# A third set of expert weights on chip, placed over finished token residuals, in an attention and mixture-of-experts kernel

## The chip, the cores and the metric

The kernel runs on one core of one Trainium2 chip. The metric is device microseconds (us) for one execution of the whole program. A core has five engines with a queue of instructions each: PE multiplies matrices, DVE (vector), ACT (scalar) and POOL (GpSimd) work element by element, and SP only issues transfers. A transfer (DMA) is issued by an engine's queue and then carried out by 16 DMA engines that all queues share. Each queue runs its instructions in order: an instruction that waits holds up all that stand behind it.

## What is computed

The input is 2048 tokens of 512 channels (8 sequences of 256). First a long convolution of key-value products with a query, summed per head, is added to x. Then comes a mixture of 16 experts, of which each token takes four, at most 256 tokens to an expert, and a shared expert that all tokens take. Cut to what matters:

```python
x = x + ssm_attention(ctx, ctx, layernorm(x), ssm_kernel, D)
h = layernorm(x)                                   # (2048, 512)
scores = softmax(h @ gate_w.T); topk_w, topk_i = top_k(scores, 4)
buf, wbuf = tokens and weights of each expert      # (16, 256), the rest is padding
xg   = h[buf]                                      # gather
mid  = silu(xg @ w_gate) * (xg @ w_up)             # (16, 256, 352)
eout = (mid @ w_down) * wbuf                       # (16, 256, 512)
y    = zeros.at[buf].add(eout)                     # scatter with addition
x    = x + y + (silu(h @ sw_gate) * (h @ sw_up)) @ sw_down
```

All numbers are f32.

## The kernel before

The order of the instructions of each engine is the order in which the program writes them; nothing is moved by a scheduler.

**The attention.** `xs` (line 102) keeps the residual x of all 16 tiles of 128 tokens in SBUF, [128, 16, 512]. A loop over the 16 tiles (line 724) computes the attention and adds it to `xs`. The shared expert is written as generators (`shared_block`, line 142): pieces of its work are put between other work with `fill(count)`. For a tile it ends with an addition to `xs` (line 195) and a transfer from there to `out` (line 196). After that the tile of `xs` isn't read again. The tiles are finished in the order 1, 0, 2, 3 and then in pairs (line 699).

**The routing** (lines 858 to 963) runs while the shared expert's last blocks (tiles 10 to 15) fill PE. In it the weights of experts 0 and 1 are asked for (line 936, four transfers each on SP's queue: gate, up, and down in two parts; `load_expert`, line 845), and later the table of the routing weights, `prob`, is written to DRAM beside the normalised tokens (`xw_d<-prob`, line 957, SP's queue). The gathers read that table too.

**An expert's tokens** take this way: `find` (line 906) computes its list of tokens on PE and DVE. `gather` (line 965) issues two indirect transfers on POOL's queue. `shuffle` (line 976) sends the result to DRAM (`slots`) and fetches it in another order (`gb`, four transfers), on SP's queue, each waiting for the one before. `tokens` (line 989) turns it on DVE to `xgT`. Three experts' tokens are under way at once (AHEAD is 3).

**The expert loop** (line 1095) does, for expert e: `gate_up` (PE, ACT, DVE); `pack` of expert e+1 (line 1002: ACT copies the columns of its last, narrow block to `wt`, so it waits for that expert's gate and up weights); `tokens(e+1)`; `find` and `gather` of expert e+3; `down` twice (line 1063), once for each half of the 256 slots. Each `down` ends with a scaling to `eo_sb` on DVE (three buffers) and an indirect transfer on POOL's queue that adds to `out` in DRAM (line 1076); below it is called the scatter. The scatters all write `out`, so each of them waits until the one before has landed. At the end of the iteration SP gets the loads of expert e+2 and then `shuffle` of expert e+3:

```python
        if e + 2 < E:
            experts[e + 2] = load_expert(e + 2)
        if e + AHEAD < E:
            moved[e + AHEAD] = shuffle(gathered[e + AHEAD])
```

The weights stand in a pool of two buffers (line 838), so the load of e+2 goes where expert e was, and waits for PE's `gate_up` and `down` of e.

Of the kernel before, what the change touches and what calls it, by code (L numbers as in the profile page):

```python
# [8 lines left out]
F32 = mybir.dt.float32  # L9
# [11 lines left out]
P = 128  # L21
BK = 32
B, S, L = 8, 256, 512
HD = 8
NC = L // P
# [5 lines left out]
E, K, CAP, I, IS = 16, 4, 256, 352, 704  # L31
# [22 lines left out]
def ssm_attention__then__moe_kernel(  # L54
# [47 lines left out]
    xs = keep.tile([P, NT, L], F32, name="xs")  # L102
# [157 lines left out]
    with ExitStack() as att:  # L260
# [441 lines left out]
        def fill(count):  # L702
            while count and behind:
                try:
                    next(behind[0])
                    count -= 1
                except StopIteration:
                    behind.pop(0)
# [15 lines left out]
        for n in range(NT):  # L724
            more = n + 1 < NT
            swift = n + 1 in SWIFT
            t = seq[n]
# [110 lines left out]
    wpool = ctx.enter_context(tc.tile_pool(name="wpool", bufs=2))  # L838
# [3 lines left out]

    NI = -(-I // P)

    def load_expert(e):
        w = wpool.tile([P, 2, NC, I], F32, name="w")
        wd = wpool.tile([P, NI, L], F32, name="wd")
        full = I // P * P
        nc.sync.dma_start(out=w[:, 0], in_=w_gate[e].rearrange("(p c) f -> p c f", p=P))
        nc.sync.dma_start(out=w[:, 1], in_=w_up[e].rearrange("(p c) f -> p c f", p=P))  # L850
        nc.sync.dma_start(
            out=wd[:, 0 : I // P, :], in_=w_down[e, 0:full, :].rearrange("(c p) f -> p c f", p=P)
        )
        nc.sync.dma_start(out=wd[0 : I - full, I // P, :], in_=w_down[e, full:, :])
        return w, wd
# [32 lines left out]
            tok.unsqueeze(2).broadcast_to([P, NT, E, 3]),  # L888
        )

    AHEAD = 3
    idx = route.tile([P, E, NSL], I32, name="idx")
    ido = route.tile([P, E, NSL], I32, name="ido")

    def compare(e):

        hot = ffn.tile([P, NT, P], BF16, name="hot", bufs=1)
        nc.vector.tensor_tensor(
            hot,
            pos[:, :, e : e + 1].broadcast_to([P, NT, P]),  # L900
            slot_f.unsqueeze(1).broadcast_to([P, NT, P]),
            ALU.is_equal,
        )
        return hot

    def find(e, hot):


        ip = ps_sm.tile([P, NSL * 3], F32, name="ip", tag="sm")
        for i in range(NT):  # L910
            nc.tensor.matmul(
                ip,
                lhsT=hot[:, i, :],
                rhs=what[:, i, e].rearrange("p n k -> p (n k)"),
                start=(i == 0),
                stop=(i == NT - 1),
            )
        info = route.tile([P, NSL, 3], F32, name="info", bufs=2)
        nc.vector.tensor_copy(info, ip.rearrange("p (n k) -> p n k", k=3))
        who = route.tile([P, NSL], F32, name="who", bufs=2)  # L920
        gap = route.tile([P, NSL], F32, name="gap", bufs=2)
        nc.vector.tensor_scalar(gap, info[:, :, 2], -1.0, 1.0, ALU.mult, ALU.add)
        nc.vector.scalar_tensor_tensor(
            who, info[:, :, 0], float(S), info[:, :, 1], ALU.mult, ALU.add
        )

        nc.vector.scalar_tensor_tensor(
            info[:, :, 1], gap, float(S), info[:, :, 1], ALU.mult, ALU.add
        )
        nc.vector.scalar_tensor_tensor(  # L930
            ido[:, e, :], info[:, :, 1], float(B), info[:, :, 0], ALU.mult, ALU.add
        )
        nc.vector.tensor_mul(gap, gap, empty)
        nc.vector.tensor_add(idx[:, e, :], who, gap)  # L934

    experts = {e: load_expert(e) for e in range(2)}
    fill(1)
    hots = {0: compare(0)}

# [18 lines left out]
    fill(2)  # L958
    for e in range(1, AHEAD):
        hots[e] = compare(e)  # L960
        fill(3)
        find(e, hots.pop(e))
    hots[AHEAD] = compare(AHEAD)

    def gather(e):
        g = ffn.tile([P, NSL, ROW], F32, name="g", bufs=AHEAD - 1)
        for n in range(NSL):
            nc.gpsimd.indirect_dma_start(  # L968
                out=g[:, n, :],
                out_offset=None,  # L970
                in_=xw_d[:, :],
                in_offset=bass.IndirectOffsetOnAxis(ap=ido[:, e, n : n + 1], axis=0),
            )
        return g

    def shuffle(g):


        slots = dram.tile([CAP, L], F32, name="slots", bufs=2)
        nc.sync.dma_start(out=slots.rearrange("(n q) f -> q n f", n=NSL), in_=g[:, :, 0:L])  # L980
        gb = ffn.tile([P, NSL * NB, P], F32, name="gb", bufs=AHEAD - 1)
        for i in range(NB):
            nc.sync.dma_start(
                out=gb[i * BK : (i + 1) * BK],
                in_=slots[:, i * P : (i + 1) * P].rearrange("(j b) f -> b j f", b=BK),
            )
        return gb

    def tokens(e):

        gb, g = moved.pop(e), gathered.pop(e)
        wg = ffn.tile([P, NSL], F32, name="wg")
        for n in range(NSL):
            nc.vector.tensor_copy(wg[:, n : n + 1], g[:, n, L + e : L + e + 1])
        xgT = ffn.tile([P, NC, CAP], F32, name="xgT")
        for n in range(NSL):
            transpose_blocks(xgT[:, :, n * P : (n + 1) * P], gb[:, n * NB : (n + 1) * NB])
        return xgT, wg
# [3 lines left out]
    def pack(w):  # L1002

        wt = ffn.tile([P, NC, 6 * Q], F32, name="wt", bufs=1)
        a, b = NW * P, NW * P + 2 * Q
        for lo, cols in ((0, slice(a, b)), (P, slice(b, I))):
            n = cols.stop - cols.start
            nc.scalar.copy(
                wt[:, :, lo : lo + 2 * n].rearrange("p c (k f) -> p c k f", k=2),
                w[:, :, :, cols].rearrange("p k c f -> p c k f"),  # L1010
            )
        return wt
# [50 lines left out]
    def down(e, n, mid, wd, wg):  # L1063
        po = ps_ex.tile([P, L], F32, name="eo", tag="ex")
        for k, f in enumerate((NW, *range(NW))):
            m = min(P, I - f * P)
            nc.tensor.matmul(  # L1067
                po,
                lhsT=mid[:m, f, n * P : (n + 1) * P],
                rhs=wd[:m, f, :],  # L1070
                start=(k == 0),
                stop=(k == NW),
            )
        o = ffn.tile([P, L], F32, name="eo_sb", bufs=3)
        nc.vector.tensor_scalar_mul(o, po, wg[:, n : n + 1])  # L1075
        nc.gpsimd.indirect_dma_start(  # L1076
            out=out,
            out_offset=bass.IndirectOffsetOnAxis(ap=idx[:, e, n : n + 1], axis=0),
            in_=o,
            in_offset=None,  # L1080
            compute_op=ALU.add,
        )

    gathered, moved = {}, {}
    for e in range(AHEAD - 1):
        gathered[e] = gather(e)
# [3 lines left out]
    wt_next = pack(experts[0][0])  # L1090
    gathered[AHEAD - 1] = gather(AHEAD - 1)
    moved[AHEAD - 1] = shuffle(gathered[AHEAD - 1])
    while behind:
        fill(1)
    for e in range(E):
        w, wd = experts.pop(e)
        wt = wt_next
        xgT, wg = xgT_next
        mid = ffn.tile([P, NI, CAP], F32, name="mid")
        if e + 1 < E:  # L1100
            gate_up(xgT, mid, w, wt, slice(0, CAP))
            wt_next = pack(experts[e + 1][0])
            xgT_next = tokens(e + 1)
            if e + AHEAD < E:
                find(e + AHEAD, hots.pop(e + AHEAD))
                gathered[e + AHEAD] = gather(e + AHEAD)
            for n in range(NSL):
                down(e, n, mid, wd, wg)
            if e + AHEAD + 1 < E:
                hots[e + AHEAD + 1] = compare(e + AHEAD + 1)  # L1110
        else:

            gate_up(xgT, mid, w, wt, slice(0, P))
            gate_up(xgT, mid, w, wt, slice(P, CAP), (NW,))
            down(e, 0, mid, wd, wg)
            gate_up(xgT, mid, w, wt, slice(P, CAP), range(NW))
            down(e, 1, mid, wd, wg)
        if e + 2 < E:
            experts[e + 2] = load_expert(e + 2)
        if e + AHEAD < E:  # L1120
            moved[e + AHEAD] = shuffle(gathered[e + AHEAD])

# [37 lines left out]
```

## Time and profile before

| | us |
|---|---|
| three runs: median, lowest, highest | 694.14, 691.29, 695.07 |
| the profiled execution, its own time | 693.31 |
| its span, first to last instruction | 691.6 |
| PE busy (matmuls) | 657.2 (95%) |
| weight loads of PE busy | 488.1 (71%) |
| DVE, ACT, POOL busy | 386.1, 185.1, 314.8 |

The times of the trace below are in microseconds from the start of the span. The attention lasts until about 357, the routing with the rest of the shared expert until 423, the sixteen experts until the end. The DMA engines move 117.79 MB, 170 GB/s on average over the span. An expert's weights are 704 + 704 + 512 + 192 KB, 2112 KB together. A group's line in the page has the line of the code, the engine, what is written and read, the count, and the time; a line of waits has who waited, for what, and then the total in us, how often, and the longest. In the timeline the number in brackets is the idle time of the engine before the instruction, and what ended it.

### The profile page before, as it was taken

To read this page: it belongs to the slowest core of one execution; us is meant where nothing else is said; L and a number is where in the kernel's file an instruction comes from. 1 tells how busy PE (TensorE), PEld (TensorE's weight loads), DVE (VectorE), ACT (ScalarE), POOL (GpSimd) and SP (SyncE) were. 2 spreads that over 40 slices of the span, in tenths; PEclk is the share of its full clock that TensorE was granted. 3 is DMA by queue.
4 is the path that set the end of the run, shared out by engine and by line. 5 is a ranking of instruction groups with operands and counts; after the bars stand their busy time and mean duration, and the time that the engine had idled before them with its cause. 6 is when DMAs were issued, how large, how long until landed. Compare 5 with 4: busy or idle time off the path is not lost. (4 is left out here: it accounts for less than half of the span.)

```text
span 691.6 us, 9761 instructions
## 1 busy us (share of the span) xinstructions
PE 657.2 (95%) x3310; PEld 488.1 (71%) x3310; DVE 386.1 (56%) x932; ACT 185.1 (27%) x465; POOL 314.8 (46%) x477
## 2 busy tenths in 40 slices
PE   7889999998999999999999999999999999899891
PEld 5667977777867877877868686766677777676670
DVE  4946666878877776676645611455455444443320
ACT  2454343444342342422322010111111111111110
POOL 5667547777685676546210310223344333332121
PEclk9999999999999999999999999999999999999997
DMA  5783454555557535441018461698999999889943
GB/s 128 244 234 99 130 160 110 159 134 149 147 143 181 146 94 150 113 108 45 16 59 274 122 188 31 207 264 254 260 267 257 254 254 251 250 254 279 266 85 44
DMA packets 98438, 117.79 MB, mean 170 GB/s; under 512 B 11267, under 2 KB 64355, under 8 KB 98388
## 3 DMA queue, kind: packets, MB, share of 16 engines
q1 hardware_dynamic: 90932, 99.86, 48.9%
q0 software_dynamic: 7168, 17.04, 12.5%
q10 hardware_dynamic: 288, 0.26, 0.3%
q8 instruction: 26, 0.43, 0.3%
q14 instruction: 24, 0.20, 0.1%
HBM read 84.25 MB, written 32.88 MB: 169 GB/s over the span
## 5 line engine op out<-in xcount | busy, mean ns | idle before, releaser
L468 PE MATMUL y<-kv,toep 128*128 128x288 f32 x528 | 140.9, 411 | 3.1 <-DVE f L518 2.7
L468 PEld LDWEIGHTS y<-kv,toep 128*128 128x128 f32 x528 | 100.0, 192 | 34.6 <-issue 7.7
L1076 POOL DMA_INDIRECT out<-eo_sb,idx x32 | 56.2, 1756 | 147.1 <-DMA wd<-in_L_ffn_w_down 73.6
L1025 PE MATMUL pgu<-xgT,w 128*128 128x256 f32 (+1 forms) x544 | 113.5, 367 | 0.0
L1025 PEld LDWEIGHTS pgu<-xgT,w 128*128 128x128 f32 x544 | 98.6, 190 | 12.9 <-issue 0.5
L1067 PE MATMUL eo<-wd,mid 128*128 128x512 f32 (+1 forms) x192 | 86.4, 598 | 0.0
L520 POOL TENSOR_TENSOR f<-f 128x256 f32<-128x256 f32 x60 | 43.8, 729 | 92.7 <-DVE f L518 87.4
L445 POOL TENSOR_TENSOR kv<-k 128x256 f32<-128x256 f32 x126 | 84.9, 706 | 0.0
L168 PE MATMUL sgu<-xnT,swg 128*128 128x256 f32 (+1 forms) x400 | 78.4, 339 | 0.4 <-DVE tail L162 0.4
L168 PE MATMUL sgu<-xnT,swu 128*128 128x256 f32 (+1 forms) x400 | 77.9, 338 | 0.0
L968 POOL DMA_INDIRECT g<-xw_d,ido x32 | 36.7, 1146 | 85.4 <-DVE idx L934 43.8
L185 PE MATMUL so<-swd,smid 128*128 128x512 f32 x160 | 73.9, 593 | 0.0
L168 PEld LDWEIGHTS sgu<-xnT,swg 128*128 128x128 f32 x400 | 65.8, 192 | 8.1 <-DVE tail L162 0.6
L168 PEld LDWEIGHTS sgu<-xnT,swu 128*128 128x128 f32 x400 | 64.6, 191 | 6.3
L1067 PEld LDWEIGHTS eo<-wd,mid 128*128 128x128 f32 (+1 forms) x192 | 35.2, 189 | 38.1 <-issue 34.8
L1033 DVE TENSOR_TENSOR mid<-eact,pgu 128x256 f32<-128x256 f32 (+1 forms) x34 | 13.8, 406 | 75.9 <-ACT eact L1032 72.8
L491 DVE TENSOR_TENSOR y<-y,again 128x576 f32<-128x576 f32 x28 | 21.4, 766 | 57.7 <-PE y L468 44.8
L185 PEld LDWEIGHTS so<-swd,smid 128*128 128x128 f32 x160 | 29.9, 190 | 31.9 <-issue 30.4
L177 ACT ACTIVATE act<-sgu 128x256 f32<-128x256 f32 (+1 forms) x50 | 17.1, 341 | 123.4 <-PE sgu L168 123.4
L518 DVE TENSOR_TENSOR f<-y,z 128x512 f32<-128x512 f32 x64 | 44.3, 692 | 6.6 <-DVE y L517 0.5
L517 DVE TENSOR_TENSOR y<-y,q 128x512 f32<-128x512 f32 x64 | 44.8, 699 | 2.2
L1075 DVE TENSOR_SCALAR eo_sb<-eo,wg 128x512 f32<-128x512 f32 x32 | 24.0, 749 | 34.8 <-PE eo L1067 23.6
(172 smaller groups left out, 794.6 us busy)
## 6 DMA issues: line engine op xcount, KB each, us to landing
w<-in_L_ffn_w_gate SPq DMA_DIRECT2D x16, 704.0 KB, 7.4
w<-in_L_ffn_w_up SPq DMA_DIRECT2D x16, 704.0 KB, 9.2
toep<-win_d SPq DMA_DIRECT2D x28, 320.0 KB, 4.4
wd<-in_L_ffn_w_down SPq DMA_DIRECT2D x16, 512.0 KB, 10.2
slots<-g SPq DMA_DIRECT2D x16, 512.0 KB, 5.7
gb<-slots SPq DMA_DIRECT2D x64, 128.0 KB, 4.9
got<-sent SPq DMA_DIRECT2D x26, 256.0 KB, 3.0
xs<-in_x SPq DMA_DIRECT2D x16, 256.0 KB, 7.1
```

Of the source, the lines that this page charges most:

```text
L168: nc.tensor.matmul(pgu[:, k, :], lhsT=sw[:, c, f * P : (f + 1) * P], rhs=toks[:, c, :], start=(c == 0), stop=(c == NC - 1),)
L185: nc.tensor.matmul(po, lhsT=m[:, i * P : (i + 1) * P], rhs=swd[:, (f - 1) % (NF + 1), :], start=(f == 0), stop=(f == NF),)
L445: (nc.vector if c in helped else nc.gpsimd).tensor_mul(kv[:, c, 0 : ND * HB].rearrange("p (d w) -> p d w", d=ND), kh[:, c, 0:HB].unsqueeze ...
L468: nc.tensor.matmul(out, lhsT=toep[:, m * P : (m + 1) * P], rhs=rhs, start=(n == 0), stop=(n == len(pairs) - 1),)
L517: nc.vector.tensor_mul(yd, yd, view(qq, 0, [[qc, 2], [B, ND], [1, HB]]))
L518: nc.vector.tensor_add(f, yd, z[:, :, :, BACK : BACK + HB])
L520: adder.tensor_add(f[:, :, 0:2, :], f[:, :, 0:2, :], f[:, :, 2:4, :])
L968: nc.gpsimd.indirect_dma_start(out=g[:, n, :], out_offset=None, in_=xw_d[:, :], in_offset=bass.IndirectOffsetOnAxis(ap=ido[:, e, n : n + 1 ...
L1025: nc.tensor.matmul(pgu[:, k, cols], lhsT=w[:, k, c, f * P : (f + 1) * P], rhs=xgT[:, c, cols], start=(c == 0), stop=(c == NC - 1),)
L1067: nc.tensor.matmul(po, lhsT=mid[:m, f, n * P : (n + 1) * P], rhs=wd[:m, f, :], start=(k == 0), stop=(k == NW),)
L1075: nc.vector.tensor_scalar_mul(o, po, wg[:, n : n + 1])
L1076: nc.gpsimd.indirect_dma_start(out=out, out_offset=bass.IndirectOffsetOnAxis(ap=idx[:, e, n : n + 1], axis=0), in_=o, in_offset=None, comp ...
```

## The change

The third set of buffers is cut from `xs`: its tiles 0 to 5 hold gate and up, its tiles 6 to 8 hold down. Experts 2, 5, 8, 11 and 14 use it; the others go on using the pool of two. All three sets are asked for in the routing, and in the loop the load is now that of e+3, at the same place on SP's queue, ahead of the same `shuffle`.

```diff
+    AHEAD = 3
+    OLD = -(-2 * NC * I // L)
+    old_w = xs[:, 0:OLD, :].rearrange("p t l -> p (t l)")[:, 0 : 2 * NC * I]
+    old_w = old_w.rearrange("p (k c f) -> p k c f", k=2, c=NC)
+    old_wd = xs[:, OLD : OLD + NI, :]
+
     def load_expert(e):
-        w = wpool.tile([P, 2, NC, I], F32, name="w")
-        wd = wpool.tile([P, NI, L], F32, name="wd")
+        if e % AHEAD < AHEAD - 1:
+            w = wpool.tile([P, 2, NC, I], F32, name="w")
+            wd = wpool.tile([P, NI, L], F32, name="wd")
+        else:
+            w, wd = old_w, old_wd
...
-    AHEAD = 3
     idx = route.tile([P, E, NSL], I32, name="idx")
...
-    experts = {e: load_expert(e) for e in range(2)}
+    experts = {e: load_expert(e) for e in range(AHEAD)}
     fill(1)
...
-        if e + 2 < E:
-            experts[e + 2] = load_expert(e + 2)
         if e + AHEAD < E:
+            experts[e + AHEAD] = load_expert(e + AHEAD)
             moved[e + AHEAD] = shuffle(gathered[e + AHEAD])
```

## The prediction

> **What bounds the kernel now.** I read the page first: its slices show where an engine has room.
>
> ```profile
> PE   7889999998999999999999999999999999899891
> ...
> DMA  5783454555557535441018461698999999889943
> ```
>
> A slice is 17.3 us. PE is full nearly everywhere; beside the start and slice 10, it isn't in slices 35 and 38 (around 597 and 648) and 40, the end. The DMA engines are nearly idle in slices 19 to 21 (around 337) and 25 (around 423), and full from slice 27 (450) to slice 38 (657). A table of stretches gives them a share of 0.89 from 433 to 566 and 0.91 from 566 to 650, at 255 GB/s.
>
> PE's timeline dates the experts by their first matmul group. Up to expert 10 each starts 15.50 us after the one before, with no gap. Three starts of the late ones:
>
> ```profile
> 596.03 1.09 PE L1037 MATMUL pgu<-xgT,wt 128*64 128x128 f32 x16 [1.95 <-ACT wt L1008]
> ...
> 645.08 1.09 PE L1037 MATMUL pgu<-xgT,wt 128*64 128x128 f32 x16 [2.15 <-ACT wt L1008]
> 660.09 1.09 PE L1037 MATMUL pgu<-xgT,wt 128*64 128x128 f32 x8
> ```
>
> These are experts 11, 14 and 15; expert 13 has a third gap, of 0.76. Together PE loses 1.95 + 0.76 + 2.15 = 4.86 us to `wt`, the packing of the next expert's weights. The waits from 430 on say what `wt` waited for, and name a second line:
>
> ```profile
> ACT wt L1008 <- DMA w<-in_L_ffn_w_up: 31.5, 8, 6.2
> POOL out L1076 <- DMA out<-eo_sb,idx: 28.1, 8, 8.8
> ```
>
> So weights come late from expert 8 on. But PE isn't what ends last: its last matmul group ends at 676.7, the span at 691.6. POOL's scatters end it, one after the other:
>
> ```profile
> 644.90 1.58 POOL L1076 DMA_INDIRECT out<-eo_sb,idx  x1 [8.76 <-DMA out<-eo_sb,idx]
> 650.60 1.56 POOL L1076 DMA_INDIRECT out<-eo_sb,idx  x1 [4.12 <-DVE mid L1059]
> 660.65 1.56 POOL L1076 DMA_INDIRECT out<-eo_sb,idx  x1 [8.49 <-issue]
> 666.26 1.56 POOL L1076 DMA_INDIRECT out<-eo_sb,idx  x1 [4.04 <-DMA out<-eo_sb,idx]
> ```
>
> Counted back from the last of the 32, these are the second of expert 12, both of 13, and the first of 14; three more follow at 671.85, 677.44 and 683.14. The names behind the arrows aren't to be believed here: DVE had the second result of expert 13 in `eo_sb` at 644.95, and its scatter went out at 660.65. What it waited for is the scatter before. The distances show the price of one: 5.61, 5.59, 5.59, 5.70 us where nothing else moves, and 10.05 us from 650.60 to 660.65. In that stretch SP's last load runs (the timeline of SP's queue; times of issue):
>
> ```profile
> 378.32 0.38 SPq L957 DMA_DIRECT2D xw_d<-prob  x1
> ...
> 433.53 0.37 SPq L849 DMA_DIRECT2D w<-in_L_ffn_w_gate  x1
> ...
> 649.62 0.38 SPq L849 DMA_DIRECT2D w<-in_L_ffn_w_gate  x1
> ```
>
> The loads of experts 2 to 15 go out at 433.5, 450.0, 465.5, 482.8 and so on to 633.3 and 649.6: some 16.6 us apart, against PE's 15.5. SP's queue has `slots` and `gb` between two loads and waits for each; POOL's has two scatters and two gathers per expert. This loop of transfers runs slower than PE and falls behind by about a microsecond per expert. The late weights and the late scatters both come of it.
>
> **The change, part by part.**
>
> *The loop.* In an iteration SP still issues one expert's loads, `slots` and `gb`, in that order and behind the same PE work (the buffer that comes free is expert e's before and after). Only the number on the weights changes: at 433.5 go the weights of 3, at 633.3 those of 15. Bytes, waits and the loop's pace up to about 649 stay as they are, since by then neither SP nor POOL waits for PE. I put the loop at no change. Every expert's weights come one turn, 16 us, earlier, and the longest wait for them was 6.2: all `wt` gaps go, which moves PE by 4.86 us.
>
> *What is late next for PE.* `gb` isn't any earlier: DVE waited for it 0.62 us at 590.06 and 1.05 at 639.83. Without the gaps expert 13 starts at 423.54 + 13 x 15.5 = 625.0, and wants the tokens of 14 from 635.8 on; they land at 639.8 as before. DVE's two turns (1.31) end at 641.1, where PE would start expert 14 at 640.3: 0.8 lost. `eo_sb` waits for scatters rise from 3.7 to about 4 us; DVE has about 5 us before the next product of `down` is due, so I put them at 0. Expert 15 then starts at about 656.4 for 660.1, and PE ends 3.7 earlier.
>
> *The tail.* This decides. The load at 649.6 no longer exists, so the scatter of 650.60 runs like the four after it, at 5.7 us for 10.05. A gain of 4.35: the last scatter goes out at 678.8 for 683.14. Does PE deliver in time? The last two results were on DVE at 670.6 and 676.7; 3.7 earlier they are at 666.9 and 673.0, and the chain wants them at 673.1 and 678.8. So the scatters stay the end, with 6 us of room, and PE's own gain is not what counts. From below: if the old load cost that scatter nothing (`gb` of expert 15, still there, were what slowed it) the gain is 0; the scatter at 644.90 ran under those same `gb` fetches in 5.70, so I don't take that. From above: 10.05 less 5.59, 4.46.
>
> *The third load in the routing.* Four more issues, about 2 us of SP's queue from 368.5, where SP idles until 378.3. Their buffers are free: the transfers of tiles 0 to 9 to `out` were issued by 321, and the loads of 0 and 1 ahead don't wait either. What they cost is bandwidth (columns: busy us of PE, its weight loads, DVE, ACT, POOL, then the clock, the DMA share, GB/s):
>
> ```profile
> 374.00:376.00 2.00, 2.00 (x11) 1.74 (x11) 1.08 (x3) 0.00 (x0) 0.00 (x0) 1.00 0.99 398
> 376.00:378.00 2.00, 2.00 (x11) 1.77 (x10) 1.31 (x5) 0.38 (x1) 0.00 (x0) 1.00 0.83 271
> 378.00:380.00 2.00, 2.00 (x11) 1.77 (x10) 0.29 (x1) 0.38 (x1) 0.00 (x0) 1.00 0.31 36
> 380.00:382.00 2.00, 2.00 (x11) 1.76 (x10) 1.96 (x2) 0.01 (x1) 0.00 (x0) 1.00 0.32 34
> ```
>
> The first two loads are through at about 377.7, at 373 GB/s in the four rows from 368 to 376. Then the `prob` table goes alone: issued at 378.3, landed 3.0 us later. By this row alone it would land at 381.3 again. The Trainium skill (DMA: Bandwidth & Descriptors, "Queues, rings and completion order") speaks against that: a queue has one ring on each DMA engine, and descriptors are consumed in ring order, so `prob` stands behind all of the third load. That is 2.163 MB at 373 GB/s, 5.8 us, to 383.5, and `prob` lands at 386.5. No row of before has it behind a load, so I take the rule. POOL's first gathers then go out at 387.8 and 389.3 for 382.59 and 384.12, and land 4.3 later (the median of that stretch), at 393.6; `slots` goes at 393.6 for 390.08, as SP was held until then by the transfer of tile 12. `gb` is 3.5 late. DVE began the turns of expert 0's tokens at 400.41 without a wait; now at about 403.9, done at 405.2, then the delayed `smid` product (0.42, due at 403.40) at 405.6. Queued behind it are DVE's later products, and PE wants that product's PSUM buffer for the block that starts at 406.24: 0.6 us to spare. By the row alone nothing is late; by the rule 3.5 of some 4.1 us of cover are used. I take 0. Beyond the cover each microsecond moves all experts. With the rate of the expert stage (255 GB/s, 8.5 us) the load ends 2.7 later: a stall of 2.1. Below zero is excluded, as nothing is taken away here.
>
> **Sum.** Against the profiled execution: span 691.6 - 4.35 = 687.25, its time 693.31 - 4.35 = 688.96. The median of the runs lies 0.83 above the profiled one; from it, 694.14 - 4.35 = 689.8.
>
> **Rivals.**
> 1. *As above*, 689.8, a chance of 0.6 with about 1 us to either side. For it: the scatters' even spacing once the loads are over, and their lag behind `eo_sb`.
> 2. *The routing eats part of the gain*: the cover of 4.1 us is too short by 1 to 3 us, since gathers and `slots` are stretched as well. 691 to 693, chance 0.22.
> 3. *The loop gets quicker too*: the 2.1 MB moved to idle time shorten the lag of the scatters before 650. Against it: the load is taken from the end of the sequence only. If the scatters of expert 13 found the one before landed 3 us sooner: 686.8. Chance 0.11.
> 4. *Slower, by the routing's chain.* `prob`, gather, `slots` and `gb` follow one another, and each lengthens to what it is from 560 to 600: the load at that stage's rate makes `gb` 6.2 late (3.5 + 2.7), a gather takes 7.6 for 4.3, `slots` 6.1 for 4.6, `gb` 5.7 for 3.1: 13.6 in a row, less 4.1 of cover 9.5 on PE and on every expert after. Less the gain of 4.35 that is 5.15, or 699.3. From 8.5 us of lateness of `gb` on the change loses. Against it: only `prob` is behind the load; the gathers start when it has passed. Chance 0.07.
> That the third load is held back by its buffer is excluded by the tiles' dates.
>
> **How the numbers follow.** A measurement of this kernel can tell about 0.5%, 3.5 us, from no change: below 690.7 is faster, above 697.6 slower. Case 1 lies mostly below 690.7 (0.5 of its 0.6) and case 3 wholly: 0.62 with rounding. Case 2 and the rest of 1: 0.31. Case 4: 0.07. The range runs from 686.8, case 3, to 693.0, the far end of case 2.
>
> **What would show it.** Right: no `wt` gap of PE; loads at the same times up to 633, none at 649; the scatter of 650 followed after 5.7; `prob` landing at 386 and PE at the first expert still at 423.5; PE's end 12 us or more ahead of the span's. Wrong: the first expert starts late (case 2 or 4); the scatters before 650 shift (case 3, or the loop is coupled to PE after all, and then the whole late stage is other than I read it); or a gap of PE that waits for `gb` of more than 1 us, enough to leave the scatters without work.

## The result, and the profile after

The changed kernel takes 688.29 us (median of 21 runs, 683.70 to 693.70) against 691.46 for the kernel before beside it (21 runs, 688.85 to 697.10): a ratio of 0.995 with a 95% interval of 0.9927 to 0.9974. That is 3.2 us less. Measured twice more beside other kernels, the ratio was 0.9962 (0.9944 to 0.998) and 0.9946 (0.9923 to 0.9968). The forecast was a step of 4.35 us; the measured one is 1.8 to 5.0 us by the first interval.

The two profiled executions differ by more, 691.6 to 684.4 us of span. Of that, 1.5 us lies ahead of the change: the first expert starts at 422.04 for 423.54, and the routing's first load stands 59.32 and 59.33 us ahead of it. Over all profiled runs the first expert starts anywhere from 419.7 to 424.2 (but for one that stalls ahead of it, below). And neither is a median run of its kernel: the profiled execution of the kernel before took 693.31 us, 1.9 above its median, that of the kernel after 686.16, 2.1 below. So the traces show where time went, and the medians how much; positions are given from here on as distances from the first expert's start, where they are compared.

PE of the kernel after, the same three experts as before (11, 14, 15):

```profile
592.51 1.09 PE L1046 MATMUL pgu<-xgT,wt 128*64 128x128 f32 x16
...
638.52 1.26 PE L1046 MATMUL pgu<-xgT,wt 128*64 128x128 f32 x16
...
653.70 1.09 PE L1046 MATMUL pgu<-xgT,wt 128*64 128x128 f32 x8
```

No idle time in brackets is left, and the list of waits no longer has the packing of the weights in it. Expert 15 starts 231.66 after the first for 236.55: 4.89 us earlier. And the scatters:

```profile
642.20 1.58 POOL L1085 DMA_INDIRECT out<-eo_sb,idx  x1 [8.37 <-DMA out<-eo_sb,idx]
647.89 1.56 POOL L1085 DMA_INDIRECT out<-eo_sb,idx  x1 [4.11 <-issue]
653.54 1.56 POOL L1085 DMA_INDIRECT out<-eo_sb,idx  x1 [4.08 <-DVE eo_sb L1084]
659.45 1.56 POOL L1085 DMA_INDIRECT out<-eo_sb,idx  x1 [4.35 <-issue]
```

The second line is the scatter that took 10.05 us beside the last load. Now it takes 5.65, as no load runs there. A table of stretches of the kernel after shows it from the other side (the last two numbers of a row are the DMA share and GB/s; the same stretch of the kernel before had 0.95 and 275):

```profile
650.00:660.00 10.00, 10.00 (x63) 7.33 (x62) 3.75 (x8) 1.09 (x4) 2.11 (x2) 1.00 0.44 55
```

The last scatter is issued 254.13 us after the first expert's start for 259.60: 5.47 us less, of which 4.40 are this one step and 1.21 lie in the chain ahead of it, less 0.14 behind it.

In the routing, the table of the routing weights and the first gather (SP's queue and POOL's, kernel after):

```profile
376.83 0.38 SPq L966 DMA_DIRECT2D xw_d<-prob  x1
...
393.14 0.38 SPq L989 DMA_DIRECT2D slots<-g  x1
```

```profile
386.27 1.80 POOL L977 DMA_INDIRECT g<-xw_d,ido  x1 [28.43 <-DMA xw_d<-prob]
```

The gather waits 9.44 us from the table's issue, for 4.27 before. DVE turns the first tokens 24.12 us after that issue for 22.09; it waited 1.95 for `gb`. PE lost nothing by it.

### The profile page after: what moved, and what is told of

The parts are those of the page before. It is cut to its first block, busy times and chain, and to the rows that moved or that the text cites. A ratio compares the mean times of both kernels' runs of the same rounds, so it can differ in the third digit from the quotient of the medians.

```text
span 684.4 us, 9764 instructions
## 1 busy us (share of the span) xinstructions
PE 656.0 (96%) x3310; PEld 487.6 (71%) x3310; DVE 385.1 (56%) x932; ACT 184.2 (27%) x465; POOL 317.7 (46%) x477
## 5 line engine op out<-in xcount | busy, mean ns | idle before, releaser
L1034 PE MATMUL pgu<-xgT,w 128*128 128x256 f32 (+1 forms) x384 | 78.2, 362 | 0.0
L977 POOL DMA_INDIRECT g<-xw_d,ido x32 | 38.2, 1193 | 84.4 <-DVE idx L943 43.4
L1034 PEld LDWEIGHTS pgu<-xgT,w 128*128 128x128 f32 x384 | 68.2, 190 | 8.7 <-issue 0.5
L1076 PE MATMUL eo<-wd,mid 96*128 96x512 f32 (+1 forms) x132 | 59.4, 598 | 0.0
L1042 DVE TENSOR_TENSOR mid<-eact,pgu 128x256 f32<-128x256 f32 (+1 forms) x34 | 13.8, 405 | 77.2 <-ACT eact L1041 72.6
L1063 ACT ACTIVATE eact<-pgu 32x128 f32<-32x128 f32 x32 | 8.5, 267 | 129.6 <-PE pgu L1054 124.0
L1076 PEld LDWEIGHTS eo<-wd,mid 96*128 96x128 f32 (+1 forms) x132 | 24.1, 189 | 26.0 <-issue 23.8
```

Source lines behind the costliest of these rows:

```text
L977: nc.gpsimd.indirect_dma_start(out=g[:, n, :], out_offset=None, in_=xw_d[:, :], in_offset=bass.IndirectOffsetOnAxis(ap=ido[:, e, n : n + 1 ...
L1034: nc.tensor.matmul(pgu[:, k, cols], lhsT=w[:, k, c, f * P : (f + 1) * P], rhs=xgT[:, c, cols], start=(c == 0), stop=(c == NC - 1),)
L1076: nc.tensor.matmul(po, lhsT=mid[:m, f, n * P : (n + 1) * P], rhs=wd[:m, f, :], start=(k == 0), stop=(k == NW),)
```

## The experiments

Twelve more measurements were made, of nine other kernels (one of them twice) and, twice, of the changed one, each beside the kernel before on the same chip. "Last scatter" is the issue of the last scatter after the first expert's start, in the one profiled execution.

| kernel | median, us | before beside it | ratio (95% interval) | last scatter |
|---|---|---|---|---|
| before | | | | 259.60 |
| after | 688.29 | 691.46 | 0.9950 (0.9927 to 0.9974) | 254.13 |
| after, again | 688.78 | 691.41 | 0.9962 (0.9944 to 0.9980) | 258.46 |
| after, a third time | 686.63 | 691.10 | 0.9946 (0.9923 to 0.9968) | 254.15 |
| before, no last load | 688.91 | 691.41 | 0.9962 (0.9939 to 0.9985) | 253.58 |
| before, no middle load | 685.75 | 690.56 | 0.9935 (0.9908 to 0.9961) | 253.34 |
| last load late | 685.17 | 691.41 | 0.9926 (0.9891 to 0.9961) | 253.99 |
| last load late, again | 685.58 | 691.10 | 0.9909 (0.9880 to 0.9939) | 253.72 |
| third load in the loop | 685.87 | 691.10 | 0.9942 (0.9915 to 0.9969) | 254.42 |
| PE + 18 matmuls | 689.95 | 691.63 | 0.9975 (0.9949 to 1.0002) | 258.06 |
| PE + 46 matmuls | 702.50 | 691.63 | 1.0161 (1.0120 to 1.0201) | 270.74 |
| third load twice | 695.69 | 691.63 | 1.0066 (1.0034 to 1.0098) | 258.79 |
| four sets | 684.70 | 691.41 | 0.9909 (0.9883 to 0.9935) | 255.11 |
| four sets, tokens first | 685.57 | 691.10 | 0.9929 (0.9906 to 0.9952) | 253.92 |

The theory at the start was the prediction's: the gain is the tail, one scatter that no load stretches any more. The rival: the gain is PE's, whose gaps are gone.

**Two sets, without the last load.** The kernel before with

```diff
-            experts[e + 2] = load_expert(e + 2)
+            experts[e + 2] = load_expert(e + 2) if e + 2 < E - 1 else (w, wd)
```

> The kernel before, two sets of weights, with the load of expert 15 left out: that expert computes with the weights of expert 13 that still lie in the same buffers, so 2.1 MB are not read. If the tail decides, this gains what the change gained, 4.4 us of span against the kernel before, though the gaps of PE ahead of experts 11, 13 and 14 (4.9 us in all) stay. If PE's gaps decide, the gain is 0 to 1 us.

Two of PE's three gaps stayed (PE of this kernel, experts 13 and 14):

```profile
624.15 1.09 PE L1037 MATMUL pgu<-xgT,wt 128*64 128x128 f32 x16 [0.83 <-ACT wt L1008]
641.01 1.09 PE L1037 MATMUL pgu<-xgT,wt 128*64 128x128 f32 x16 [1.77 <-ACT wt L1008]
642.03 3.54 PE L1045 MATMUL pgu<-xgT,wt 128*128 128x256 f32 x8
```

They are 2.60 us of 4.86, and the last line shows another loss: eight records took 3.54 us, for 1.99 at the expert ahead, as the granted clock was 0.58 and 0.57 in the rows from 642 to 646 (more on this at the third load twice, below). So expert 15 starts 235.93 after the first, only 0.62 earlier than in the kernel before. Yet the kernel gains what the change gained: 0.9962, the same as the changed kernel measured beside it. The scatter at the old place of the last load took 5.62 us. That speaks for the tail, and against PE. But PE is no longer far behind it here. The last two scatters went out 0.28 us after their results, and the last step is 6.15 us:

```profile
675.36 1.55 POOL L1076 DMA_INDIRECT out<-eo_sb,idx  x1 [4.59 <-DVE eo_sb L1075]
```

**More work on PE.** The changed kernel, with matmuls that nobody reads ahead of the last expert's own (18, and 46):

```diff
+            more = ps_sm.tile([P, CAP], F32, name="more", tag="sm")
+            for i in range(18):
+                nc.tensor.matmul(more, lhsT=w[:, 0, 0, 0:P], rhs=xgT[:, 0, :], start=True, stop=True)
             gate_up(xgT, mid, w, wt, slice(0, P))
```

> The changed kernel with 18 matmuls of 128x256 more on PE ahead of the last expert's own, whose results nobody reads: 18 x 0.216 = 3.9 us. If the scatters are the end and PE has 5 us of room there (last result in eo_sb at 671.1, last scatter at 676.2), the time is that of the changed kernel within 0.5 us. If PE's time counts, it is 3.9 us longer.

> The same with 46 matmuls, 9.9 us. With 5.1 us of room the time grows by 4.8 us against the changed kernel, and the last two scatters follow eo_sb at once instead of the scatter before; if PE's time counts in full, by 9.9 us.

The dose was mis-sized: an f32 matmul of this form leaves two records (18 left 36), so one costs 0.44 us and not 0.216. PE and POOL of the kernel with 18:

```profile
653.42 7.93 PE L1123 MATMUL more<-xgT,w 128*128 128x256 f32 x36
```

```profile
672.79 1.56 POOL L1085 DMA_INDIRECT out<-eo_sb,idx  x1 [6.69 <-DVE eo_sb L1084]
```

7.9 us of PE work cost 0.9 to 2.0 us by the ratios (0.9975 against 0.9962 and 0.9946), and 20.0 us with 46 matmuls cost 13.8 to 14.9. Both leave PE about 6 us of room (7.9 - 2.0 to 7.9 - 0.9; 20.0 - 14.9 to 20.0 - 13.8). With the room used up, the scatter waits for `eo_sb`, as the second line shows, and no longer for the one before. So PE isn't the end, and the 4.9 us that it gained are room, not time.

**The last load at its old place.** The changed kernel, with expert 15's load alone back at the end of expert 13's turn:

```diff
         if e + AHEAD < E:
-            experts[e + AHEAD] = load_expert(e + AHEAD)
+            if e + AHEAD < E - 1:
+                experts[e + AHEAD] = load_expert(e + AHEAD)
             moved[e + AHEAD] = shuffle(gathered[e + AHEAD])
+        if e + 2 == E - 1:
+            experts[E - 1] = load_expert(E - 1)
```

> The changed kernel, but the weights of expert 15 alone are asked for where they were before, at the end of expert 13's turn; all others stay one turn early. If the gain is the tail (the last load stretching one scatter by 4.35 us), it is gone: the scatter issued beside that load takes about 10 us for 5.65, PE still has no gaps for the packed weights of experts 11 to 14, and the time is that of the kernel before less at most 1.2 us (the part of the chain before that load). If the gain is PE's vanished gaps (4.9 us), most of it stays: 3 to 5 us below the kernel before.

> The changed kernel with expert 15's load alone at its late place, once more. It was 6.2 us below the kernel before, 3 below the changed kernel, against the theory of the tail. If that stands, it is 5 to 7 us below the kernel before again, and the second scatter of expert 12 goes out some 4 us earlier after the first expert's start than in the changed kernel; if it was a matter of few runs, it comes out with the changed kernel, 2 to 4 us below the kernel before.

The theory of the tail expected the gain to go. It stayed, in both measurements. POOL of the first of them, scatters of expert 12 and 13:

```profile
634.32 1.62 POOL L1085 DMA_INDIRECT out<-eo_sb,idx  x1 [1.44 <-DMA out<-eo_sb,idx]
640.85 1.58 POOL L1085 DMA_INDIRECT out<-eo_sb,idx  x1 [4.90 <-DVE xgT L404]
647.18 1.56 POOL L1085 DMA_INDIRECT out<-eo_sb,idx  x1 [4.75 <-issue]
655.30 1.56 POOL L1085 DMA_INDIRECT out<-eo_sb,idx  x1 [6.56 <-issue]
```

The load now runs from 643.3 on, and the steps are 6.53, 6.33 and 8.12 us. In the changed kernel the load ran in the first of them: 9.99, 5.69, 5.65. The sums are 20.98 and 21.33; in the kernel before, which has a load in the first and in the last, 26.14. So a load costs the chain about the same in either place. That suggests that what counts is only that there is one less.

**Two sets, without a middle load.** That made another test: take away a load where nothing ends. The kernel before with its two sets as fixed tiles, and

```diff
     def load_expert(e):
+        w, wd = sets[e % 2]
+        if e == 8:
+            return w, wd
```

> The kernel before, two sets of weights, with the load of expert 8 left out instead of that of expert 15: expert 8 computes with the weights of expert 6. The same 2.1 MB are missing, but in the middle of the full stretch, where the scatters lag behind eo_sb by only some 3 us. If what counts is that no load runs beside the last scatters, the second scatter of expert 13 still comes about 10 us after the first, the lag that was saved in the middle is built up again, and the time is 0 to 1.5 us below the kernel before. If what counts is how many bytes the full stretch carries, it gains at least what leaving out the last load gained (2.5 us by the medians), and the scatters of expert 12 stand 3 us or more earlier than in the kernel before.

```profile
635.23 1.58 POOL L1082 DMA_INDIRECT out<-eo_sb,idx  x1 [9.61 <-DVE eo_sb L1081]
640.88 1.56 POOL L1082 DMA_INDIRECT out<-eo_sb,idx  x1 [4.07 <-DVE mid L1061]
650.94 1.56 POOL L1082 DMA_INDIRECT out<-eo_sb,idx  x1 [8.49 <-issue]
656.59 1.56 POOL L1082 DMA_INDIRECT out<-eo_sb,idx  x1 [4.08 <-DVE mid L1039]
```

The scatter beside the last load still takes 10.06 us, and still the kernel gains 4.8 us. The chain stands 5.9 us earlier than before already at the second scatter of expert 12 (215.49 for 221.36 after the first expert's start), and that lead isn't lost again: the last scatter comes 6.3 earlier. PE's gaps went here too (0.25 us is left), but the last two scatters went out 4.8 and 4.2 us after their results, so PE isn't what they waited for. The narrow theory falls here. By the end of the loop the chain of scatters no longer waits for results, so what shortens a step of it in that stretch can come off the end, and here it did. Two things stay untested: the fixed tiles without the missing load, and the changed kernel with one load more in the full stretch.

**The third load elsewhere.** The changed kernel with only two loads in the routing, and the third in the loop's first turn, ahead of expert 3's.

```diff
+        if e == 0:
+            experts[AHEAD - 1] = load_expert(AHEAD - 1)
         if e + AHEAD < E:
```

> The changed kernel with three sets of weights and the last load at its early place, but the third set's load isn't moved into the routing: it is issued in the first turn of the loop, just ahead of expert 3's, so from 432 on the DMA engines carry as many bytes as in the kernel before. If the gain is that no load runs beside the last scatters, it stays: the scatter of 648 is followed after 5.7, and the time is that of the changed kernel within 1 us (some 3 us below the kernel before). If the gain is the 2.1 MB that were moved out of the full stretch, the scatters before 648 come 3 to 8 us later, and the time is that of the kernel before, or above it.

The gain stayed, but the run doesn't decide what it was made for. The third set's buffers wait for nothing, so SP issued that load 1.4 us after the first expert's start, and it ran in the 8 idle us ahead of the next load at 10.0, not in the full stretch. What it shows: the routing isn't needed as a place. The last scatter (254.42) is where the changed kernel has it.

**The third load twice.** The changed kernel with

```diff
     experts = {e: load_expert(e) for e in range(AHEAD)}
+    load_expert(AHEAD - 1)
```

> The changed kernel with the third expert's load issued twice in a row in the routing, into the same buffers (the second copy changes nothing in them). The table of the routing weights stands behind both on SP's queue. If it waits its turn there, it lands about 6 us later than in the changed kernel (at about 389 for 384), the tokens of expert 0 come 6 us later, the cover of about 2.2 us that is left there is used up, and PE stalls some 3.8 us before the experts: the time is 3 to 5 us above the changed kernel. If the table is served beside the load instead, it lands at the same time and nothing is late: within 0.5 us.

Against the first load's issue, the gather came 7.05 us later than in the changed kernel and the turns of the first tokens 7.93; the first expert 66.95 for 59.32, a stall of 7.63. The table itself was issued 7.88 us later (21.99 us behind the first load's issue for 14.11): the second copy goes into the same buffers, and SP waited 5.9 us for the first to land. From issue to gather it was 8.61 us, for 9.44 in the changed kernel. So the run shows what lateness costs, and is no test of the order within the ring. The time is 1.0 to 1.2% above the changed kernel (1.0066 against 0.9946 to 0.9962), some 7 to 8 us, where 3 to 5 were expected. DVE and PE:

```profile
407.73 1.30 DVE L404 STREAM_TRANSPOSE xgT<-gb 128x512 f32<-128x512 f32 x2 [9.88 <-DMA gb<-slots]
```

```profile
409.39 3.72 PE L168 MATMUL sgu<-xnT,swg 128*128 128x256 f32 x8 [5.64 <-DVE smid L179]
412.95 1.89 PE L168 MATMUL sgu<-xnT,swu 128*128 128x256 f32 x8
```

The cover was 7.93 less 5.64, 2.3 us, as expected. The rest, 2.0 us, is mostly PE's clock. After the pause the same eight matmul records take 3.72 us for 1.89, and the granted clock of these stretches was (the number before the DMA share)

```profile
408.00:410.00 2.00, 0.60 (x2) 0.52 (x3) 1.67 (x4) 0.00 (x0) 0.00 (x0) 0.50 0.31 121
410.00:412.00 2.00, 2.00 (x6) 1.64 (x5) 0.00 (x0) 0.00 (x0) 0.00 (x0) 0.50 0.99 245
412.00:414.00 2.00, 2.00 (x8) 1.65 (x8) 0.00 (x0) 0.00 (x0) 0.00 (x0) 0.77 1.02 329
```

The Trainium skill (TensorE: Matmul & The Clock Gate, "Part 1: The HAM clock gate (the "warmup" mystery)") states that after an idle window of about 3.4 us TensorE runs at half clock until it has been busy for about as long. The rows agree for this pause of 5.64 us: 0.50, and 0.77 in the row in which it ends. But shorter pauses had the same price in other places: 1.77 us without the last load, 2.39 in the changed kernel measured again, and 2.47 at a late expert of this run. Behind each the clock was at half for about 3.4 us (without the last load 0.65, 0.50, 0.50 and 0.64 in the four rows of 1 us from 642 to 646). The gaps of 1.95 and 2.15 us in the kernel before had none: 1.00 in the rows behind both. So a pause under 3.4 us isn't safe here, and what decides whether it costs is not shown.

**Four sets.** The changed kernel with a fourth set over `xnT`, whose load goes out behind the last residual tile; in the loop the load is that of e + 4.

```diff
+    turned_w = flat[:, 0 : 2 * NC * I].rearrange("p (k c f) -> p k c f", k=2, c=NC)
+    turned_wd = flat[:, 2 * NC * I : 2 * NC * I + NI * L].rearrange("p (n l) -> p n l", n=NI)
...
+    experts[SETS - 1] = load_expert(SETS - 1)
     for e in range(E):
...
-        if e + AHEAD < E:
-            experts[e + AHEAD] = load_expert(e + AHEAD)
+        if e + SETS < E:
+            experts[e + SETS] = load_expert(e + SETS)
```

> The changed kernel with a fourth set of weights, in the space of the transposed tokens that the shared expert has finished with: expert 3's load is issued at about 422, behind the last residual tile, into 8 us in which the DMA engines move little, and in the loop the load is that of expert e + 4. The loads then end one turn earlier, at about 631 for 645. If lag of the scatters behind eo_sb is what is left at the end, they run at 5.6 us each from then on and catch up with PE, whose last result is at 671: the last scatter is issued at about 671 to 672 for 676.2, 4 to 5 us below the changed kernel. If PE's own work is the bound after the change: no gain, within 0.5 us.

> Four sets of weights as in the run before with four, but in the loop SP issues the tokens' way of expert e + 3 (slots, gb) ahead of the load of expert e + 4. If all that counts is how many loads run beside the scatters and when the last of them ends, this is no better than four sets with the load first, or worse, as its last load starts near 630 for 614: 5 to 7 us below the kernel before. If the order on SP's queue holds the loop back, since slots waits behind a load, it is 2 us or more better than that.

With the load first: 0.9909, and 0.9962 for the changed kernel measured beside it, 3.7 us less. These two intervals don't meet, so four sets beat the change in this measurement. With the tokens' way first (the two `if` parts exchanged): 0.9929, no better, as expected, and its interval meets that of the changed kernel beside it (0.9946). The profiled execution of the first doesn't show the gain: its last scatter comes at 255.11, and the chain didn't catch up with PE, whose last result was in `eo_sb` 5.6 us earlier. Three of its scatters took 3.7 us to issue (last section); whether that is why is not shown.

**The changed kernel again.** It ran beside the others, twice.

> The changed kernel once more, beside the others. Both theories: 3 to 5 us below the kernel before.

> The changed kernel beside them: 2 to 4 us below the kernel before.

Its three profiled executions have the last scatter at 254.13, 258.46 and 254.15. The steps beside the old load's place are the same in all (5.65, 5.41 and 5.67), but the second scatter of expert 12 comes at 220.16, 224.46 and 219.83. The late one has its last two loads 2 and 4 us late, and two gaps of PE that wait for tokens, 1.22 and 2.39. So the loop's own pace varies by 4 us from one execution to the next, about what the change is worth. Last load late (0.9926 and 0.9909) lies below the changed kernel (0.9962 and 0.9946) in both measurements, but the intervals meet in each, and the traces differ by less than half a microsecond, the late one aside. Whether it is truly faster stays open.

## Why the prediction came out as it did

*The loop.* Right for the loads: in the profiled execution the last one of the changed kernel goes out 208.6 us after the first expert's start for 209.7 of the load that it takes the place of. The chain up to the second scatter of expert 12 stands 1.2 us earlier than before in that execution, 3.1 later in the second: that is neither a gain nor a loss that these runs can tell.

*PE's gaps.* All went. `gb` was the next to be late, as forecast: DVE waited 2.90 us for it at expert 14 and PE ran from there a touch late (231.66 for an ideal 231.5). The forecast of 0.8 lost was 0.2. PE gained 4.89 where 3.7 was said (its own terms, 4.86 less 0.8, give 4.06). In the second execution of the changed kernel two gaps for tokens stood in place of the old ones, 1.22 and 2.39, and expert 15 started at 237.87, later than before. The second is the gap of over 1 us that was named as a sign of being wrong. But the scatters were not left without work: the last went out 3.2 us after its result.

*The tail.* The step was sized right: 10.05 to 5.65, a gain of 4.40 where 4.35 was said, and with 6 us of room for PE, which the added matmuls measured as about 6. By the medians the step is 2.6 to 4.5 us in three measurements; 4.35 lies inside the first's and the third's interval (1.8 to 5.0; 2.2 to 5.3), and just outside the second's (1.4 to 3.9). That difference is smaller than the loop's own spread, and no run names a cause for it. The absolute forecast of 689.8 came near 688.29 with some luck: it was counted from the median of three runs, 694.14, which lay 2.7 above the median of all 21, and the step from it was 1.2 larger than measured.

*The routing.* The trace agrees with the rule of ring order: the DMA engines carry the load until about 383, and the first gather goes out at 386.27. Without the third load in the routing (it was in the loop instead) it followed the table's issue after 4.26 us, as in the kernel before. The gathers were 5.17 us late (5.2 said), `slots` 4.55 (3.5 said), but `slots` then landed faster, and the tokens were 2.03 late for 3.5. The cover sufficed: PE lost nothing (59.32 for 59.33).

*What was wrong in the reasoning* is the weight on the end. "The tail. This decides" and, against the third rival, "the load is taken from the end of the sequence only", made the place the cause. Leaving out a load in the middle gained as much or more (0.9935) with the last load still in place, and a last load in its late place cost the gain nothing. What the runs show in its stead: late in the full stretch each load stretches one scatter of its turn to 10 or 11 us from 5.7, or two or three of them by less, and the chain there no longer waits for results. So one load fewer in that stretch is worth 5.5 to 6.3 us in the traces where the loop kept its pace, against the one trace of the kernel before, and 2.5 to 4.8 us by the medians, at both places where it was taken out. The third rival's argument, that moving bytes out of the loop can be worth something beside the end, was set aside too soon; in the changed kernel itself, though, the scatters ahead of the last load's place were not clearly earlier (1.2 and 1.5 us in two executions, 3.1 later in one). The change moved one load out of it, into the routing. That the end of the sequence is where it is missed is how the change happens to do it.

## What to carry to other kernels

Look for the chain that has fallen behind its data: here the results of the last eight scatters were ready 5.7 to 16 us before these could go, so the microseconds of their own steps counted, and PE's gaps did not, as long as that lead lasted. What such a chain competes with should be moved into idle stretches of the same resource; the place where the saving shows in the trace needn't be the place that earned it, and only an edit somewhere else tells. Where a kernel's own runs spread by as much as the change is worth, count on several profiles and many runs before a last microsecond is believed.

## What the runs showed of the hardware

A pause of PE of 5.64 us cost 7.6, as the clock came back at half, and pauses of 1.77, 2.39 and 2.47 us were followed by half clock for about 3.4 us as well, while 1.95 and 2.15 were not. And POOL's issue of a scatter took 3.7 us for 1.6 in several runs, each time while DVE's comparison of `pos` with the slots ran. In the kernel after, POOL and DVE:

```profile
609.24 3.71 POOL L1085 DMA_INDIRECT out<-eo_sb,idx  x1 [9.17 <-DMA wd<-in_L_ffn_w_down]
```

```profile
609.21 2.28 DVE L907 TENSOR_TENSOR hot<-pos,slot_f 128x2048 bf16<-128x2048 f32 x1
```

It happened at up to three places of an execution, depending on how the two meet. Not every meeting costs: in the kernel with four sets a scatter at 560.52 took 1.57 us with the comparison running throughout. Nor does the whole 2.1 us stay in the chain: the scatter above and the next took 8.29 and 8.77 us to the one behind, and 5.79 and 10.47 in the third execution of the changed kernel, where the first of them was issued quickly. That leaves 0.8 us. No run was made to test it.
